# Graph attention in two layers: one multiplication of each step moved from VectorE to GpSimd

## The chip, the core and the metric

The kernel runs on one core of a Trainium2 chip. The core has five engines with queues of their own: TensorE (PE: matmuls; PEld: its weight loads), VectorE (DVE), ScalarE (ACT), GpSimd (POOL) and SyncE (SP, which only issues transfers). Each engine executes its instructions in the order of its own queue and waits at an instruction until the semaphores named there have been reached. The metric is the device time of one execution in microseconds (us); less is better.

## The reference

The input is a set of 2708 tokens of width 512 and a sparse, symmetric 0/1 matrix that says which tokens are neighbours. Two layers of the same form follow each other, each with weights of its own:

```python
q, k, v = h @ Wq.T + bq, h @ Wk.T + bk, h @ Wv.T + bv     # 8 heads of 64
scores  = einsum('nhd,mhd->hnm', q, k) / 8
scores  = where(adj + eye == 0, -1e9, scores)
ctx     = einsum('hnm,mhd->nhd', softmax(scores), v)
h1      = layer_norm(h + ctx @ Wo.T + bo)
h2      = layer_norm(h1 + relu(h1 @ W1.T + b1) @ W2.T + b2)   # 2048 inside
```

All values are float32. A token has few neighbours, at most some twenty, itself included, so almost all scores are masked.

## The kernel before

**Attention by lists.** The kernel does not form the matrix of scores. It first makes a list of neighbours for each token and sorts the tokens by the length of the list, so that the 22 tiles of 128 tokens have lists of bounded length (`CAPS`, from 22 slots in tile 0 to 3 in the last). A slot stands for one neighbour of each of the 128 tokens. The keys and values of all tokens of a layer lie in a table in HBM (`kv_d`), a row of 1024 numbers for each token, keys first.

**Steps.** A tile is worked off in steps of up to two slots. One step consists of these instructions:

- GpSimd issues one gather for each slot (`loads`, L1228; the instruction has the line L1099): 128 rows of the table come into a `kv` buffer.
- `weights` (L1134): VectorE multiplies the keys by the query (L1136, two slots in one instruction) and sums each head (L1142), which gives the scores `sc`.
- `weigh` (L1149): ScalarE takes the exponential of the scores (L1155, one instruction a slot), which gives the weights `p`. ScalarE multiplies the second slot's values with their weights, head by head, in eight instructions (L1162). VectorE multiplies the first slot's values with theirs in one instruction (L1168). In a tile's first step (`s0 == 0`) the products go to the sum `acc`; in every later step they stay in the `kv` buffer, and VectorE then adds them to `acc` (L1175).

When a tile is through, VectorE adds the two halves of the sum and reduces the weights (`sums`, L1179), and ScalarE divides (`divided`, L1206), which gives `cx`, the tile's context.

**Order of the work.** The order is written out by hand: each engine executes its instructions in the order in which the Python code emits them. `attend` (L1582) is a generator that emits a step at a time. In step k it first takes the next buffer, for which the gathers of step k+3 are emitted (`EARLY = 3`), then emits `weights` of step k and then `weigh` of step k-1, so that ScalarE has a step's time for the exponentials. In layer 1 a `kv` buffer is one of seven. `advance` (L1641) draws steps from this generator between the matmuls of another block, at a pace written in `PACE`, and `until` (L1653) draws what is still missing of a tile when its context is needed.

**Blocks.** Two tiles make a block; the feed-forward runs block by block (`feed_forward`, L1447), 16 stages `f` of four matmuls `pf` (L1494) and, three stages later, two matmuls `a` (L1467). During the feed-forward of one block the attention of later tiles is computed. At stage f = 10 TensorE transposes the context of the next block's first tile and at f = 11 that of its second (`flip`, `tp` L1273), projects both (`o`, L606), and VectorE adds the residual and normalises (`norm`, L1253; its reciprocal root `rd`, L1263, is on GpSimd). After the last stage VectorE adds the block's result `a` to the residual (L1532) and normalises again, and in layer 1 GpSimd scatters the rows to the output (`put`, L1062).

So GpSimd's queue holds gathers, the `rd` of every normalisation and the scatters, all in one order.

Of the kernel before, what the change touches and what calls it, by code (L numbers as in the profile page):

```python
# [480 lines left out]
def by_edges(ctx: ExitStack, tc: tile.TileContext, x, xT, adj, layers, out, redo):  # L481
# [9 lines left out]
    nc = tc.nc  # L491
# [142 lines left out]
    def size(g):  # L634
        return min(P, N - g * P)
# [472 lines left out]
    def asked(n, g):  # L1108

        r = size(g)  # L1110
        if g in own:
            return own.pop(g)
        if n == 0 and not all_made:
            return None
        q = at.tile([P, DM], F32, tag="q", name="q", bufs=QB)
        fetch(n, q, q_d[n], g)
        return q

    def chunks_of(g):
        S = CAPS[g]  # L1120
        k = (S + SLOTS - 1) // SLOTS
        cuts = [-(-S * i // k) for i in range(k + 1)]
        return [(g, a, b - a) for a, b in zip(cuts, cuts[1:])]

    class Tile:


        def __init__(self, g, q):
            self.g, self.r, self.q = g, size(g), q
            self.sc = at.tile([P, LIST, NH], F32, tag="sc", name="sc", bufs=2)  # L1130
            self.p = at.tile([P, LIST, NH], F32, tag="p", name="p", bufs=2)
            self.acc = None
# [16 lines left out]
        def weigh(self, kv, s0, c):  # L1149
            r, g, p = self.r, self.g, self.p  # L1150
            if s0 == 0:
                self.acc = at.tile([P, SLOTS, DM], F32, tag="acc", name="acc", bufs=2)
                self.wide = c
            for s in range(s0, s0 + c):
                nc.scalar.activation(  # L1155
                    p[:r, s, :], self.sc[:r, s, :], AF.Exp, bias=minus[:r, g, s : s + 1]
                )
            to = self.acc[:r] if s0 == 0 else kv[:r, :, DM:]
            for i in range(1, c):
                for h in range(NH):  # L1160
                    hd = slice(h * DK, (h + 1) * DK)
                    nc.scalar.activation(  # L1162
                        to[:, i, hd],
                        kv[:r, i, DM + h * DK : DM + (h + 1) * DK],
                        AF.Copy,
                        scale=p[:r, s0 + i, h : h + 1],
                    )
            nc.vector.tensor_tensor(  # L1168
                to[:, 0, :].rearrange("p (h d) -> p h d", d=DK),
                kv[:r, 0, DM:].rearrange("p (h d) -> p h d", d=DK),  # L1170
                p[:r, s0, :].unsqueeze(2).to_broadcast([r, NH, DK]),
                ALU.mult,
            )
            if s0:
                nc.vector.tensor_tensor(  # L1175
                    self.acc[:r, :c, :], self.acc[:r, :c, :], kv[:r, :c, DM:], ALU.add
                )
# [50 lines left out]
    def loads(n):  # L1228

        ready = []  # L1230
        for g, s0, c in (chunk for g in order for chunk in chunks_of(g)):
            r = size(g)
            kv = rows_of_keys(n)
            for s in range(s0, s0 + c):
                load = gather(kv[:r, s - s0, :], kv_d[n], idx[:r, g, s : s + 1])
                for move in written[n]:
                    tc.add_manual_dep(
                        load.ins,
                        move.ins.name,
                        mybir.DependencyInfo(  # L1240
                            mybir.DependencyClass.Sync, mybir.DependencyReason.DATA
                        ),
                        reason="every row of keys is in its place",
                    )
                written[n].clear()
            ready.append(kv)
            if len(ready) > EARLY:
                yield ready.pop(0)
        yield from ready
# [332 lines left out]
    def attend(n, got):  # L1582

        peak = small.tile([P, NT], F32, tag="peak", name="peak", bufs=1)
        nc.vector.memset(peak, 0.0)
        loaded = loads(n)
        steps = []
        for g in order:
            cuts = chunks_of(g)
            steps += [(g, s0, c, i, i + 1 == len(cuts)) for i, (_, s0, c) in enumerate(cuts)]  # L1590
            if g == order[1]:
                steps += [None] * 3
        steps += [None] * 3
        kv = next(loaded)
        yield 0.0
        q = asked(n, order[0])
        done = [None] * 3
        for k, step in enumerate(steps):
            if step:
                g, s0, c, i, last = step  # L1600
                if i == 0:
                    while q is None:
                        q = asked(n, g)
                        if q is None:
                            yield None
                    t, q = Tile(g, q), None
                if k > 0:
                    kv = next(loaded)
                t.weights(kv, s0, c)
                if q is None and g != order[-1]:  # L1610
                    q = asked(n, order[order.index(g) + 1])
                done.append((t, kv, s0, c, last))
            else:
                done.append(None)
            t3, t2, t1 = done[-4:-1]
            if t1:
                t1[0].weigh(*t1[1:4])
            if t2 and t2[-1]:
                t2[0].sums(peak)
            if t3 and t3[-1]:  # L1620
                got[t3[0].g] = t3[0].divided()
            yield c / SLOTS if step else 0.2
        nc.vector.tensor_reduce(flags[:, 4 + n : 5 + n], peak, AX.X, ALU.max)
        nc.vector.tensor_scalar(
            flags[:, 4 + n : 5 + n], flags[:, 4 + n : 5 + n], SAFE, None, ALU.is_le
        )
# [30 lines left out]

    got = {}
    ahead = attend(0, got)
    early = {}  # L1660

# [39 lines left out]
    for n in range(NL):  # L1701
        last = n == NL - 1
        nxt = None if last else Layer(n + 1, layers[n + 1])
        if n > 0:
            streamed = now.queries(order[10:16])
            got = {}
            ahead = attend(n, got)
            for _ in range(2):
                now.query(*pool.pop(0))
# [178 lines left out]
```

## Time and profile before

| what | value |
|---|---|
| time, median of 3 runs | 1846.8 us (1846.43 to 1847.19) |
| time of the profiled execution | 1846.72 us, of which the span from first to last instruction is 1844.6 us |
| granted TensorE clock, mean | 0.998 |
| layer 1 in the trace | from about 1085 us to the end |
| one block of feed-forward in layer 1 | 63.7 us |
| layer 1: gathers, mean | 210 of 1222 ns (1085 to 1780 us) |
| layer 1: L1168 on the first slot's values of a later step | 89 instructions, 689 ns |
| layer 1: L1168 of a tile's first step | 22 instructions, 697 ns |

The page of a profile has the engines' busy time first, then the costliest groups of instructions with mean duration and with what ended the idle time before them. Further views are asked of the trace: the waits of one engine in a stretch of time, the instructions of one engine in order of time (the timeline; its columns are start, duration, engine, line, operation, output<-inputs, shapes and, in brackets, idle time before and what ended it), and the busy time by stretches.

### The profile page before, as it was taken

The page shows a single profiled execution, that of the slowest core. Times are in us where ns is not written, and L with a number is a line of the kernel's source. Part 1 is how long each engine was busy: PE and PEld are TensorE (multiplying, and loading weights), DVE is VectorE, ACT ScalarE, POOL GpSimd, SP SyncE. Part 2 cuts the span into 40 slices and gives each one's busy share as a digit, 9 for nine tenths or more (in the row PEclk, how much of TensorE's full clock was granted, in tenths as well). Part 3 has the DMA queues.
Part 4 walks back from the last instruction along what each step waited for, and adds up shares of the span by engine and source line. Part 5 has one row for each costly group of instructions (what it writes and reads, how often), then busy time and mean ns, then how long its engine had stood idle before and what let it go on. Part 6 is the DMA issues. An engine that isn't in the chain of part 4 may idle for free.

```text
span 1844.6 us, 20998 instructions
## 1 busy us (share of the span) xinstructions
PE 1830.8 (99%) x6205; PEld 1095.4 (59%) x6205; DVE 1374.6 (75%) x2147; ACT 944.3 (51%) x3263; POOL 782.5 (42%) x745
## 2 busy tenths in 40 slices
PE   9999999999999999999999999999999999999997
PEld 4444456565666656566565544666666666666666
DVE  5886778787777777767774148877998988899842
ACT  5770445654446555555543113655665575566531
POOL 3234755544435434443431032444563545355302
PEclk9999999999999999999999999999999999999999
DMA  9997987654646455553631676845563755456300
GB/s 345 363 335 257 373 280 247 220 161 163 205 142 230 147 188 183 176 181 106 222 121 46 230 261 258 293 140 197 177 232 140 254 195 185 180 199 209 119 1 21
DMA packets 129829, 368.01 MB, mean 200 GB/s; under 512 B 14378, under 2 KB 32670, under 8 KB 129704
## 3 DMA queue, kind: packets, MB, share of 16 engines
q0 software_dynamic: 70608, 252.12, 39.6%
q1 hardware_dynamic: 50042, 93.64, 14.3%
q10 hardware_dynamic: 9054, 20.81, 2.9%
q8 instruction: 50, 0.82, 0.2%
q14 instruction: 75, 0.61, 0.1%
HBM read 315.84 MB, written 50.68 MB: 199 GB/s over the span
## 4 chain that ended last, share of the span: by engine, by line
PE 93%; DVE 3%; ACT 1%; issue 1%; DMA 1%; POOL 0%; SPq 0%; POOLq 0%; DVEq 0%
PE pf L1494 30%; PE a L1467 29%; PE o L606 8%; PE v L606 8%; PE k L606 8%; PE q L606 7%; PE tp L1273 3%; DVE sc L1142 1%; DVE kv L1136 1%; PE a L1482 1%; ACT kv L1162 1%; DVE acc L1175 0%; DVE kv L1168 0%; ACT cx L1206 0%; DMA kv<-kv_d,listed 0%
## 5 line engine op out<-in xcount | busy, mean ns | idle before, releaser
L1494 PE MATMUL pf<-hT,w 128*128 128x256 f32 (+1 forms) x2816 | 631.7, 372 | 0.1
L1494 PEld LDWEIGHTS pf<-hT,w 128*128 128x128 f32 x2816 | 518.3, 190 | 172.8 <-issue 107.5
L1099 POOL DMA_INDIRECT kv<-kv_d,listed x420 | 507.8, 1209 | 254.2 <-issue 108.7
L1467 PE MATMUL a<-w,ft 128*128 128x512 f32 x1312 | 611.2, 592 | 0.0
L1505 ACT ACTIVATE ft<-pf,b 128x256 f32<-128x256 f32 (+1 forms) x336 | 153.9, 461 | 412.0 <-PE pf L1494 411.9
L1467 PEld LDWEIGHTS a<-w,ft 128*128 128x128 f32 x1312 | 247.0, 190 | 187.2 <-issue 165.8
L1263 POOL TENSOR_TENSOR rd<-va,mhalf 128x1 f32<-128x1 f32 (+1 forms) x88 | 81.2, 922 | 565.4 <-DVE va L1261 565.4
L1162 ACT ACTIVATE kv<-kv,p 128x64 f32<-128x64 f32 x1232 | 311.0, 335 | 5.0
L1136 DVE TENSOR_TENSOR kv<-kv,q 128x1024 f32<-128x1024 f32 (+1 forms) x222 | 257.0, 1158 | 16.5 <-DMA q<-q_d,ident_i 13.0
L1142 DVE TENSOR_REDUCE sc<-kv 128x16 f32<-128x1024 f32 (+1 forms) x222 | 258.0, 1162 | 7.6
L1175 DVE TENSOR_TENSOR acc<-acc,kv 128x1024 f32<-128x1024 f32 (+2 forms) x178 | 205.3, 1153 | 76.5 <-ACT kv L1162 65.0
L1155 ACT ACTIVATE p<-sc,listed 128x8 f32<-128x8 f32 x420 | 104.3, 299 | 123.9 <-DVE sc L1142 112.9
L1168 DVE TENSOR_TENSOR kv<-kv,p 128x512 f32<-128x512 f32 (+1 forms) x178 | 123.1, 691 | 36.2 <-ACT p L1155 36.1
L606 PE MATMUL o<-wo,cT 128*128 128x512 f32 x336 | 148.4, 594 | 0.6 <-ACT cT L1278 0.6
L606 PEld LDWEIGHTS o<-wo,cT 128*128 128x128 f32 x336 | 62.2, 190 | 72.5 <-issue 60.9
L731 DVE MAX8 tops<-code 128x8 f32<-128x247 f32 (+2 forms) x242 | 78.6, 400 | 28.5 <-ACT code L726 28.2
L1267 DVE SCALAR_TENSOR_TENSOR h<-h,rd,ln_b 128x512 f32<-128x512 f32 (+1 forms) x88 | 66.1, 751 | 41.0 <-POOL rd L1263 41.0
L1206 ACT ACTIVATE cx<-acc,su 128x64 f32<-128x64 f32 (+1 forms) x352 | 88.2, 333 | 12.9 <-DVE su L1198 7.4
L1162 ACT ACTIVATE acc<-kv,p 128x64 f32<-128x64 f32 (+1 forms) x352 | 88.8, 334 | 1.4
L1560 ACT COPY kvs<-v 128x512 f32<-128x512 f32 (+1 forms) x22 | 12.9, 585 | 137.3 <-PE v L606 136.6
L726 ACT ACTIVATE code<-aj 128x1354 bf16<-128x1354 int32 (+1 forms) x44 | 72.9, 1719 | 16.0 <-POOL aj L720 11.3
L1429 DVE TENSOR_TENSOR h<-o,xb 128x512 f32<-128x512 f32 (+1 forms) x44 | 30.2, 687 | 63.6 <-PE o L606 46.5
(183 smaller groups left out, 1605.7 us busy)
## 6 DMA issues: line engine op xcount, KB each, us to landing
aj<-in_adj SPq DMA_DIRECT2D x42, 677.0 KB, 6.4
kv_d<-kvs ACTq DMA_DIRECT2D x21, 512.0 KB, 5.5
xg<-in_xT SPq DMA_DIRECT2D x19, 512.0 KB, 7.0
w<-in_W SPq DMA_DIRECT2D x16, 512.0 KB, 7.2
kv<-kv_d,listed POOLq DMA_INDIRECT x420, 6.0
zT_d<-zT SPq DMA_DIRECT2D x22, 256.0 KB, 4.1
xb_d<-h SPq DMA_DIRECT2D x21, 256.0 KB, 6.8
q<-q_d SPq DMA_DIRECT2D x21, 256.0 KB, 4.4
```

The lines of the kernel that those rows point to most:

```text
L606: nc.tensor.matmul(o[:r], xs(c), wm[:, c, :], start=(c == 0), stop=(c == NC - 1))
L1099: return nc.gpsimd.indirect_dma_start(out=to, out_offset=None, in_=table[:, :], in_offset=bass.IndirectOffsetOnAxis(ap=s, axis=0), bounds_ ...
L1136: nc.vector.tensor_tensor(kv[:r, :c, :DM], kv[:r, :c, :DM], self.q[:r].unsqueeze(1).to_broadcast([r, c, DM]), ALU.mult,)
L1142: nc.vector.tensor_reduce(self.sc[:r, s0 : s0 + c, :], kv[:r, :c, :DM].rearrange("p s (h d) -> p s h d", d=DK), AX.X, ALU.add,)
L1155: nc.scalar.activation(p[:r, s, :], self.sc[:r, s, :], AF.Exp, bias=minus[:r, g, s : s + 1])
L1162: nc.scalar.activation(to[:, i, hd], kv[:r, i, DM + h * DK : DM + (h + 1) * DK], AF.Copy, scale=p[:r, s0 + i, h : h + 1],)
L1168: nc.vector.tensor_tensor(to[:, 0, :].rearrange("p (h d) -> p h d", d=DK), kv[:r, 0, DM:].rearrange("p (h d) -> p h d", d=DK), p[:r, s0, : ...
L1175: nc.vector.tensor_tensor(self.acc[:r, :c, :], self.acc[:r, :c, :], kv[:r, :c, DM:], ALU.add)
L1206: nc.scalar.activation(cx[:r, hd], self.acc[:r, 0, hd], AF.Copy, scale=self.su[:r, h : h + 1])
L1467: nc.tensor.matmul(a[:r, cols], fts[f][:, c0 : c0 + r], self.w2[f // 2][:, f % 2, cols], start=(f == 0), stop=(f == NFC - 1),)
L1494: nc.tensor.matmul(pf[:, :w], self.w1[f // 2][:, c, f % 2 * P : f % 2 * P + P], hT[:, c, :w], start=(c == 0), stop=(c == NC - 1),)
L1505: nc.scalar.activation(ft[:, :w], pf[:, :w], AF.Relu, bias=self.b1[:, f : f + 1])
```

## The change

The multiplication of the first slot's values with their weights is given to GpSimd where the layer is the second one (`n` is 1) and the step is not the tile's first (`s0` is not 0). All else keeps its place in the code: the instruction is emitted at the same point of `weigh`, and the addition to `acc` on VectorE follows it. A tile now knows its layer.

```diff
-        def __init__(self, g, q):
-            self.g, self.r, self.q = g, size(g), q
+        def __init__(self, n, g, q):
+            self.n, self.g, self.r, self.q = n, g, size(g), q
...
-            nc.vector.tensor_tensor(
+            by = nc.gpsimd if self.n and s0 else nc.vector
+            by.tensor_tensor(
                 to[:, 0, :].rearrange("p (h d) -> p h d", d=DK),
                 kv[:r, 0, DM:].rearrange("p (h d) -> p h d", d=DK),
                 p[:r, s0, :].unsqueeze(2).to_broadcast([r, NH, DK]),
...
-                    t, q = Tile(g, q), None
+                    t, q = Tile(n, g, q), None
```

## Prediction

> **What bounds the kernel now.** I read the busy times first, then TensorE's waits in layer 1 (the only place that the edit touches), then the groups of the two engines that trade work.
>
> ```profile
> PE 1830.8 (99%) x6205; PEld 1095.4 (59%) x6205; DVE 1374.6 (75%) x2147; ACT 944.3 (51%) x3263; POOL 782.5 (42%) x745
> ```
> ```profile
> PE tp L1273 <- ACT cx L1206: 0.7, 1, 0.7
> PE o L606 <- ACT cT L1278: 0.6, 1, 0.6
> ```
>
> TensorE is busy for 99% of the span. The second fence is all that it waits for from 1085 to 1800 us: 1.3 us. So VectorE, though full, bounds nothing today except at two places, and relieving it can return about 1.3 us, under 0.1%. A measurement of this kernel can tell about 0.2% (3.7 us) from no change. The question is what the move does to the time at which contexts (cx) reach TensorE.
>
> ```profile
> L1099 POOL DMA_INDIRECT kv<-kv_d,listed x210 | 256.5, 1222 | 78.7 <-issue 44.3 <-DVE acc L1175 9.4 <-ACT p L1155 9.1
> L946 POOL TENSOR_TENSOR kvs<-kvs,bk 128x512 f32<-128x512 f32 x20 | 25.4, 1270 | 52.6 <-ACT kvs L942 47.4 <-issue 5.2
> L1168 DVE TENSOR_TENSOR kv<-kv,p 128x512 f32<-128x512 f32 x88 | 60.7, 689 | 3.9 <-ACT p L1155 3.8
> ```
>
> **Removed.** The third row (and one of 20 partitions): 89 multiplications on VectorE by 689 ns, 61 us. They lie under TensorE's work and are worth nothing by themselves, beyond the 1.3 us.
>
> **Added.** 89 multiplications on GpSimd. No row shows this one; the nearest is L946, GpSimd's float32 128x512 instruction with two inputs: 1270 ns, 1254 to 1297 in twenty. Bounds: 0.7 us if it ran as on VectorE; 2.5 us if on top of 1270 it also sat through a VectorE instruction of 1.2 us each time. I take 1.27, and expect an error upward rather than down, because VectorE was in one-input searches while L946 ran and is in two-input work here.
>
> **Where it lands in GpSimd's queue.** In step k the queue holds the gathers of step k+3, then the multiplication of step k-1, then the gathers of k+4, and so on. The multiplication waits for ScalarE's exponential, and the addition on VectorE (L1175) now waits for the multiplication. Until now GpSimd ran ahead of VectorE, held only by free buffers; now they are tied together step by step. Behind the multiplication stand gathers, the roots rd and the scatters. The gathers stay early enough: issued about three and a half steps (15 us) ahead, where a landing takes 6. The roots don't suffer: VectorE reaches a normalisation only after the addition that needed GpSimd's last multiplication. What counts is the length of a step, so I look at the densest stretch that ends at a waiting TensorE, tile 10 of the block (7, 10). GpSimd, then VectorE, from the timeline:
>
> ```profile
> 1299.35 1.53 POOL L1099 DMA_INDIRECT kv<-kv_d,listed  x1 [0.30 <-issue]
> 1303.45 0.99 POOL L1099 DMA_INDIRECT kv<-kv_d,listed  x1 [0.30 <-issue]
> 1304.74 1.62 POOL L1099 DMA_INDIRECT kv<-kv_d,listed  x1 [0.30 <-ACT p L1155]
> 1306.67 0.99 POOL L1099 DMA_INDIRECT kv<-kv_d,listed  x1 [0.30 <-issue]
> ```
> ```profile
> 1304.28 1.23 DVE L1175 TENSOR_TENSOR acc<-acc,kv 128x1024 f32<-128x1024 f32 x1
> 1305.42 1.22 DVE L1136 TENSOR_TENSOR kv<-kv,q 128x1024 f32<-128x1024 f32 x1
> 1306.67 1.22 DVE L1142 TENSOR_REDUCE sc<-kv 128x16 f32<-128x1024 f32 x1
> 1307.81 0.68 DVE L1168 TENSOR_TENSOR kv<-kv,p 128x512 f32<-128x512 f32 x1
> 1308.60 1.23 DVE L1175 TENSOR_TENSOR acc<-acc,kv 128x1024 f32<-128x1024 f32 x1
> ```
>
> VectorE's step is now 4.32 us (addition 1304.28 to addition 1308.60). A gather takes 0.99, but 1.62 at 1304.74, when VectorE is inside an addition until 1305.51; it ends 0.85 later. Over layer 1's timeline the 68 gathers that start beside no two-input VectorE instruction take 0.99; the other 142 average 1.33 and end 0.86 (median) after it. Gaps: 0.30 between gathers, 0.03 from gather to arithmetic, 0.18 from arithmetic to gather.
>
> [...] The trace shows one direction, GpSimd waiting. The other, VectorE held by a multiplication of 1.27, it shows nowhere. [...]
>
> **The step afterwards.** Cycle of GpSimd in a step: 0.18; a first gather that meets the addition just released, 1.95 (1.23 - 0.15 + 0.86); 0.30; a second, 0.99; 0.03; multiplication 1.27. That is 4.72 us. VectorE alone would need 4.32 - 0.68 = 3.6, so GpSimd now sets the step. Walked through tile 10 (additions of its four later steps; today at 1304.28, 1308.60, 1311.85, 1316.09): the scatter ends at 1299.04, three gathers run as now to 1304.44, multiplication to 1305.74, addition 1305.77; then every 4.72: 1310.49, 1315.21, 1319.93. The last is 3.8 us late: 1.5 from the start, 0.4 from each full step, 1.5 from the step of one slot, which today is short (3.25). The sum and the context follow it.
>
> ```profile
> 1321.66 2.01 ACT L1206 ACTIVATE cx<-acc,su 128x64 f32<-128x64 f32 x8
> 1325.91 0.60 PE L1273 MATMUL tp<-ident,cx 128*128 128x128 f32 x4
> 1327.12 2.41 PE L606 MATMUL o<-wo,cT 128*128 128x512 f32 x5 [0.60 <-ACT cT L1278]
> ```
>
> The context is done at 1323.67, and TensorE takes it at 1325.91: 2.24 us of room. 3.8 - 2.24 = 1.6 us of stall. The same gap for second tiles, read in the timeline: -1.4 and 2.25 in the blocks before, 5.9, 6.9, then 10.7 and more; first tiles have 12 and more. In the next block (6, 11) the room is 5.9 + 1.6; the lag carried in is about 3, tile 6 adds 2.7 (three full steps by 0.4 and one short one by 1.5), tile 11 adds 3.8 as tile 10 did, and VectorE's idle time, 64.0 - 57.8 = 6 us in a block, recovers some of it:
>
> ```profile
> 1290.00:1354.00 64.00, 63.40 (x223) 40.69 (x222) 57.84 (x78) 39.50 (x150) 33.17 (x27) 1.00 0.58 197
> ```
>
> I take half of it: 9.5 - 7.5 would be 2.0 with no recovery, none with all; 1.0. Blocks (8, 9), with 2.25 of room, and (18, 17), with none, have short tiles and many waits on TensorE or ScalarE in between; 1.5 together. Then 1 for VectorE held by the lock, 0.5 for a multiplication somewhat over 1.27 (four steps by 0.13), and -0.6 from the relief. Later blocks have room and cost nothing. Another deadline, the addition of a block's result to the residual (L1532), which must free TensorE's accumulators 7 us into the next block, has 1.7 to 3.9 us of room after three steps; three by 0.4 fits.
>
> Sum: 1.6 + 1.0 + 1.5 + 1 + 0.5 - 0.6 = 5.0 us. The profiled execution took 1846.72 us (span 1844.6 and 2.1 around it), as good as the median of 1846.8, so the time is **1852**, slower by 0.3%.
>
> **Rivals.** *Covered:* the multiplication costs about 1.1 or less, or finds GpSimd free earlier. The place is tile 10: its four cycles then sum to less than 2.24 us of lag plus today's time, which happens from a cycle of 4.72 - (1.6 / 4) = 4.3 down, a multiplication of 0.87, or from 1.1 with half of the starting delay of 1.5 absent. For it: GpSimd is busy only 33 us in that block of 64. Against: it is idle when VectorE is, too. Time 1847, not slower.
>
> [...]
>
> *Relief wins:* VectorE's additions start sooner, the 1.3 us of waits vanish and nothing else appears: 1845.5; over 0.2% isn't there to be had, since TensorE has no more idle time in layer 1.
>
> That the multiplications don't move is excluded: the condition holds for all 89.
>
> **How the numbers follow.** Stalls of a few us as worked out: 0.46 (its own range 1849 to 1860; about one in eight of it within 0.2%). Covered: 0.24. GpSimd the bound: 0.26. Relief: 0.04. The range must leave out 2 in 10: 1846 cuts off the relief and a little of the covered case, 1875 cuts off the upper half of the bound. Slower: 0.40 + 0.26 = 0.66; within 0.2%: 0.06 + 0.24 = 0.30; faster 0.04.
>
> **What would show it.** GpSimd's new row at 1.27 to 1.5 us a piece, 89 of them; a new wait of VectorE's addition on GpSimd, some tens of us in all; the gathers still short of delaying L1136; TensorE's waits at tp and o risen from 1.3 to about 6 us, at the contexts of tiles 10 and 11. Wrong would be: a row near 2 us, TensorE waiting in every block, or no wait at all.

## The result, and the profile after

The changed kernel takes 1862.93 us (median of 6 runs, 1860.9 to 1864.96) against 1846.78 us (6 runs beside it). The ratio is 1.0087, with a 95% interval of 1.0077 to 1.0097: 16.1 us slower, inside the predicted range and on the predicted side, but three times the 5.0 us of the sum. The profiled execution took 1860.9 us (span 1859.2), so its span has grown by 14.6 us, and these are what the readings below account for. From L1168 on, line numbers are one higher than before: the multiplication is L1169, the addition L1176, the transposition tp L1274, the eviction cT L1279, the relu ft L1506, the division cx L1207.

Busy times of the span, then TensorE's waits from 1085 to 1812 us (total, times, longest):

```profile
PE 1836.0 (99%) x6205; PEld 1095.7 (59%) x6205; DVE 1325.3 (71%) x2058; ACT 943.2 (51%) x3263; POOL 918.3 (49%) x834
```
```profile
PE o L606 <- ACT cT L1279: 6.1, 6, 3.3
PE pf L1495 <- ACT ft L1506: 2.8, 2, 1.5
PE q L606 <- DMA zT<-zT_d: 0.9, 1, 0.9
PE tp L1274 <- ACT cx L1207: 0.7, 1, 0.7
```

VectorE is busy for 49 us less and GpSimd for 136 more. TensorE's waits in layer 1 have gone from 1.3 to 10.5 us, and ScalarE ends nearly all of them: evictions (cT, which copy a transposed context out of TensorE's accumulator) and relus (ft), not contexts (cx). TensorE is also busy for 5 us longer with the same instructions; a part of that is a cost of its own, below.

GpSimd's groups from 1085 to 1800 us, and VectorE's longest wait in the same stretch:

```profile
L1099 POOL DMA_INDIRECT kv<-kv_d,listed x210 | 293.4, 1397 | 56.9 <-issue 45.7 <-POOL kv L1169 3.9 <-DMA kv_d<-kvs,ident_i 3.1
L1169 POOL TENSOR_TENSOR kv<-kv,p 128x512 f32<-128x512 f32 (+1 forms) x89 | 96.5, 1085 | 34.8 <-ACT p L1155 33.2
```
```profile
DVE acc L1176 <- POOL kv L1169: 75.0, 55, 3.4
```

The multiplication takes 1085 ns on GpSimd, not 1270 (L946, the row it was taken from, stays at 1268). VectorE's additions wait for it for 75 us, a wait that did not exist. The gathers have grown from 1222 to 1397 ns (210 of them: 37 us), because their timing has changed. In tile 10 this is seen instruction by instruction, GpSimd's timeline first, then VectorE's additions:

```profile
1307.12 1.06 POOL L1169 TENSOR_TENSOR kv<-kv,p 128x512 f32<-128x512 f32 x1
1308.34 1.99 POOL L1099 DMA_INDIRECT kv<-kv_d,listed  x1 [0.16 <-POOL kv L1169]
1310.64 1.00 POOL L1099 DMA_INDIRECT kv<-kv_d,listed  x1 [0.30 <-issue]
1311.67 1.05 POOL L1169 TENSOR_TENSOR kv<-kv,p 128x512 f32<-128x512 f32 x1
```
```profile
1308.22 1.23 DVE L1176 TENSOR_TENSOR acc<-acc,kv 128x1024 f32<-128x1024 f32 x1 [2.02 <-POOL kv L1169]
1312.75 1.22 DVE L1176 TENSOR_TENSOR acc<-acc,kv 128x1024 f32<-128x1024 f32 x1 [0.92 <-POOL kv L1169]
1317.29 1.23 DVE L1176 TENSOR_TENSOR acc<-acc,kv 128x1024 f32<-128x1024 f32 x1 [1.99 <-POOL kv L1169]
1321.82 0.69 DVE L1176 TENSOR_TENSOR acc<-acc,kv 128x512 f32<-128x512 f32 x1 [0.92 <-POOL kv L1169]
```

The multiplication ends, the addition that waited for it starts at once, and the gather that starts beside that addition takes 1.99 instead of 1.00 us. The cycle is 4.53 us, the same in all three steps. So the predicted mechanism is there. TensorE's waits lie elsewhere than predicted, though; ScalarE's and TensorE's timelines of the same place:

```profile
1327.38 2.00 ACT L1207 ACTIVATE cx<-acc,su 128x64 f32<-128x64 f32 x8
1329.29 0.45 ACT L1506 ACTIVATE ft<-pf,b 128x256 f32<-128x256 f32 x1
1329.82 0.49 ACT L1155 ACTIVATE p<-sc,listed 128x8 f32<-128x8 f32 x2
1330.34 2.02 ACT L1162 ACTIVATE kv<-kv,p 128x64 f32<-128x64 f32 x8
1332.27 0.46 ACT L1506 ACTIVATE ft<-pf,b 128x256 f32<-128x256 f32 x1
1332.62 1.11 ACT L1279 ACTIVATE cT<-tp,bv 128x128 f32<-128x128 f32 x4
```
```profile
1324.60 0.60 PE L1274 MATMUL tp<-ident,cx 128*128 128x128 f32 x4
1328.48 1.28 PE L1274 MATMUL tp<-ident,cx 128*128 128x128 f32 x4
1333.03 8.83 PE L606 MATMUL o<-wo,cT 128*128 128x512 f32 x16 [3.26 <-ACT cT L1279]
```

The eviction at 1332.62 is that of tile **7**, the block's first, whose context was transposed at 1324.60 and could have been evicted from 1325.2. It stands in ScalarE's queue behind tile 10's division and behind the exponentials and copies of one more step, and these came late because VectorE's scores did. TensorE needs tile 7's eviction first (o, 1333.03). What TensorE waits for is the queue. Tile 10's own context is late as well: it is done at 1329.38, 0.9 us after its transposition began, which therefore takes 1.28 us instead of 0.60. But that costs less than the eviction does.

The span's 14.6 us by place (the lag of each matmul behind the same one before): 0.4 ahead of layer 1; 0.9 at 1127 us (a wait at q for zT, the transposed tokens, which a transfer brings; in the kernels below with moved multiplications it is none in four and up to 3.3 us in one, and nothing ties it to the change); 1.25 at block (8, 9), half of it a transposition that does wait for its context (1.31 us instead of 0.60); 5.05 at block (7, 10); 2.55 at block (6, 11); 4.45 in the blocks after. Block (7, 10) holds more than its wait. Two windows of TensorE at that place (length, busy PE, PEld, DVE, ACT, POOL, granted clock, DMA share, GB/s):

```profile
1333.00:1338.00 5.00, 4.97 (x8) 2.19 (x9) 1.44 (x2) 2.13 (x8) 0.00 (x0) 0.66 0.26 93
1338.00:1343.00 5.00, 5.00 (x16) 2.69 (x16) 3.94 (x8) 0.00 (x0) 1.00 (x1) 1.00 0.00 0
```

After the wait the granted clock is at 0.5 from 1334.43 to 1337.84: 3.41 us, in which the matmuls o follow each other at 0.85 instead of 0.43 us. That adds 1.7 us to the 3.3 of the wait.

### The profile page after: what moved, and what is told of

Read it like the earlier page. It is cut to its first block, busy times and chain, and to the rows that moved or that the text cites. A ratio compares the mean times of both kernels' runs of the same rounds, so it can differ in the third digit from the quotient of the medians.

```text
span 1859.2 us, 20995 instructions
## 1 busy us (share of the span) xinstructions
PE 1836.0 (99%) x6205; PEld 1095.7 (59%) x6205; DVE 1325.3 (71%) x2058; ACT 943.2 (51%) x3263; POOL 918.3 (49%) x834
## 5 line engine op out<-in xcount | busy, mean ns | idle before, releaser
L1099 POOL DMA_INDIRECT kv<-kv_d,listed x420 | 543.9, 1295 | 233.0 <-issue 110.9
L1506 ACT ACTIVATE ft<-pf,b 128x256 f32<-128x256 f32 (+1 forms) x336 | 153.2, 460 | 391.1 <-PE pf L1495 377.7
L1176 DVE TENSOR_TENSOR acc<-acc,kv 128x1024 f32<-128x1024 f32 (+2 forms) x178 | 205.9, 1157 | 154.9 <-POOL kv L1169 75.0
L1136 DVE TENSOR_TENSOR kv<-kv,q 128x1024 f32<-128x1024 f32 (+1 forms) x222 | 262.4, 1182 | 16.6 <-DMA q<-q_d,ident_i 13.7
L1142 DVE TENSOR_REDUCE sc<-kv 128x16 f32<-128x1024 f32 (+1 forms) x222 | 257.9, 1162 | 7.6
L1169 POOL TENSOR_TENSOR kv<-kv,p 128x512 f32<-128x512 f32 (+1 forms) x89 | 96.5, 1085 | 34.8 <-ACT p L1155 33.2
L1207 ACT ACTIVATE cx<-acc,su 128x64 f32<-128x64 f32 (+1 forms) x352 | 88.2, 333 | 13.2 <-DVE su L1199 7.7
L1169 DVE TENSOR_TENSOR kv<-kv,p 128x512 f32<-128x512 f32 (+1 forms) x89 | 61.6, 692 | 32.3 <-ACT p L1155 32.3
```

The lines of the kernel that those rows point to most:

```text
L1099: return nc.gpsimd.indirect_dma_start(out=to, out_offset=None, in_=table[:, :], in_offset=bass.IndirectOffsetOnAxis(ap=s, axis=0), bounds_ ...
L1136: nc.vector.tensor_tensor(kv[:r, :c, :DM], kv[:r, :c, :DM], self.q[:r].unsqueeze(1).to_broadcast([r, c, DM]), ALU.mult,)
L1142: nc.vector.tensor_reduce(self.sc[:r, s0 : s0 + c, :], kv[:r, :c, :DM].rearrange("p s (h d) -> p s h d", d=DK), AX.X, ALU.add,)
L1169: by.tensor_tensor(to[:, 0, :].rearrange("p (h d) -> p h d", d=DK), kv[:r, 0, DM:].rearrange("p (h d) -> p h d", d=DK), p[:r, s0, :].unsqu ...
L1176: nc.vector.tensor_tensor(self.acc[:r, :c, :], self.acc[:r, :c, :], kv[:r, :c, DM:], ALU.add)
L1207: nc.scalar.activation(cx[:r, hd], self.acc[:r, 0, hd], AF.Copy, scale=self.su[:r, h : h + 1])
```

## The experiments

Unless said otherwise, each edit is to the changed kernel, and each ratio is to the kernel before on the same chip (1846.8 to 1847.4 us). `times(engine, a, b)` stands for the multiplication of heads a to b (b not included), with two more arguments for another place to write to and to read from. The excerpts of code leave out the lines around them.

### A tie without length, and length without a tie

GpSimd multiplies one head of eight; the addition still waits for it in every step.

```diff
-            by.tensor_tensor(... all heads ...)
+            if self.n and s0:
+                times(nc.gpsimd, 0, 1)
+                times(nc.vector, 1, NH)
+            else:
+                times(nc.vector, 0, NH)
```

> GpSimd multiplies one head of eight (64 columns, about 0.2 us), VectorE the other seven (about 0.62 us). The addition waits for GpSimd as in the changed kernel. A: GpSimd's step falls to 4.53 - 0.85 = 3.7 us, VectorE's own is 4.25: 1846 to 1849 us. If being tied step by step is what costs, whatever the duration: 1855 us or more.

1847.86 us, ratio 1.0004 (0.9995 to 1.0013). The addition waits 19.7 us for GpSimd, and TensorE 1.5 us at o. The tie between the engines alone costs nothing that can be measured; what GpSimd has to do between two ties does.

Then the opposite: VectorE keeps its multiplication, and GpSimd makes an additional one of the same size on keys that are no longer needed, which nothing waits for in its step.

```diff
+            if self.n and s0:
+                times(nc.gpsimd, 0, NH, keys, keys)   # keys: kv[:r, 0, :DM]
+            times(nc.vector, 0, NH)
```

> VectorE keeps the multiplication of the first slot in both layers. GpSimd does one of the same size at the same place of its queue, but on the dead keys' products in the same buffer, so that no addition waits for it. Theory A (the addition waits for GpSimd, whose step of 4.53 us is longer than VectorE's): VectorE runs in its own step of 4.32 us again, gathers have 15 us of lead, so 1847 to 1852 us; the additions' wait on GpSimd (75 us) is gone. Theory B (what costs is VectorE held by a GpSimd instruction that reads SBUF): VectorE's two-input rows grow at least as in the changed kernel (L1136 1260 ns for 1215) and it has the 61 us of multiplications on top: 1860 us or more.

1856.92 us, ratio 1.0048 (1.0031 to 1.0064), between what the two theories expected. VectorE's groups from 1085 to 1800 us, the addition, then its own multiplication:

```profile
L1182 DVE TENSOR_TENSOR acc<-acc,kv 128x1024 f32<-128x1024 f32 x77 | 107.4, 1395 | 17.0 <-ACT kv L1162 10.0
L1171 DVE TENSOR_TENSOR kv<-kv,p 128x512 f32<-128x512 f32 x88 | 78.0, 886 | 2.3 <-ACT p L1155 2.2
```

No addition waits for GpSimd, but additions take 1395 ns (1226 before) and multiplications 886 (689): 77 x 0.169 + 88 x 0.197 = 30 us more on VectorE. The reduction L1142, with one input, stays at 1220 ns. So the additions and multiplications became longer with GpSimd's arithmetic beside them, and without a tie that loses 9.6 us. (Late gathers are not the cause: L1136 waits 2.3 us for them, 3.5 before.)

### How much of the loss is that lengthening

The multiplication is left out for these steps; GpSimd fills the place of the product with zeros, twice, to take the same time without reading anything. (From a tile's second step on, the values of first slots are thus missing from the sums.)

```diff
+            if self.n and s0:
+                nc.gpsimd.memset(to[:, 0, :], 0.0)
+                nc.gpsimd.memset(to[:, 0, :], 0.0)
```

> In place of the multiplication GpSimd fills the first slot's values with zeros, twice (two times about 0.53 us), which reads nothing; the multiplication itself is left out in layer 1 from a tile's second step on, so the output is another one. Queue, duration and the addition's wait stay as in the changed kernel. A: 1858 to 1864 us, with a step of about 4.6 us in the dense stretch. B: VectorE isn't held any more (no L1136 above 1.25 us), so at least half of the 16 us goes: 1855 us or less.

1859.81 us, ratio 1.0067 (1.005 to 1.0084), inside what theory A expected. The two fills take 540 + 524 ns, as long as the multiplication. VectorE's key multiplication and addition:

```profile
L1136 DVE TENSOR_TENSOR kv<-kv,q 128x1024 f32<-128x1024 f32 x98 | 118.9, 1214 | 2.3 <-DMA kv<-kv_d,listed 2.3
L1184 DVE TENSOR_TENSOR acc<-acc,kv 128x1024 f32<-128x1024 f32 x77 | 94.3, 1225 | 101.9 <-POOL kv L1180 63.6 <-ACT kv L1162 33.9 <-issue 2.7
```

L1136 is back at the 1215 ns it had before (1260 in the changed kernel), so the fills do not lengthen it. Of the 16 us, 12.5 remain. The lengthening is thus worth 3 us here at most, and the two intervals overlap. By place, the profiled spans differ by 2.4 us, of which 0.7 arise ahead of layer 1, where the kernels are the same, and 0.8 at zT; 1.0 arises in the late blocks and none at the three blocks named above. The rest of the loss is there with fills in place of the multiplication.

### The length of GpSimd's step

Half of the heads on each engine, by the first edit with 4 in place of 1:

> GpSimd multiplies heads 0 to 3, VectorE heads 4 to 7, with an instruction each. Theory A (the length of GpSimd's step decides): GpSimd's multiplication takes about 0.55 us, its step 0.18 + 1.99 + 0.30 + 1.00 + 0.03 + 0.55 = 4.05 us, shorter than the 4.32 of before, so only the late start of a tile's first multiplication is left: 1848 to 1852. Theory B (VectorE held, in proportion to GpSimd's time in arithmetic): half of 16 us, 1855.

1850.78 us, ratio 1.0023 (1.0013 to 1.0032), inside what theory A expected. GpSimd's timeline in tile 10, from the multiplication of its third such step to that of the fourth:

```profile
1312.85 0.62 POOL L1171 TENSOR_TENSOR kv<-kv,p 128x256 f32<-128x256 f32 x1
1313.63 1.03 POOL L1099 DMA_INDIRECT kv<-kv_d,listed  x1 [0.16 <-issue]
1314.97 1.03 POOL L1099 DMA_INDIRECT kv<-kv_d,listed  x1 [0.30 <-issue]
1316.01 0.72 POOL L1171 TENSOR_TENSOR kv<-kv,p 128x256 f32<-128x256 f32 x1
```

The step is 3.16 us here; the 4.05 expected is met only by the tile's first (4.11), in which a gather of 2.00 us still meets the addition. Here the shorter multiplication is done before VectorE reaches the addition (1313.90), so the next gather is under way by then: 1.03 us. Half of the multiplication takes away three quarters of the loss. Tile 10 shows why: the step in which VectorE waits for GpSimd pays for the collision as well (4.11 us), and the one in which it doesn't pays nothing (3.16).

Twice the multiplication, the second on the product of the first, so that values are weighted twice:

```diff
+            if self.n and s0:
+                times(nc.gpsimd, 0, NH)
+                times(nc.gpsimd, 0, NH)
```

> GpSimd executes each moved multiplication twice, the second on the product of the first, so the values are weighted twice and the output differs. Theory A: GpSimd's step is 4.53 + 1.1 = 5.6 us, 1.3 above what the step was before, in some 4 steps of a tile and 8 of a block; that is 10 us a block against an idle time of VectorE of about 10 with the relief, so also the late blocks, which have room of 6 to 13 us, begin to stall: 1880 to 1920. Theory B (the tie alone costs, whatever GpSimd's time): 1863 to 1866.

1940.5 us, ratio 1.0511 (1.0494 to 1.0529): beyond the upper end of what was expected. The cycle is 5.66 us, as expected (additions of tile 10 at 1322.80, 1328.46, 1334.11, 1339.77), and VectorE's additions wait 181 us. TensorE's waits in layer 1, the four largest:

```profile
PE pf L1503 <- ACT ft L1514: 29.7, 16, 3.8
PE o L606 <- ACT cT L1287: 15.0, 7, 3.3
PE tp L1282 <- ACT cx L1215: 9.9, 4, 4.6
PE a L1476 <- DVE h L1541: 4.4, 4, 1.3
```

Half of these 59 us are at pf, at relus. The other 35 of the 94 us are in TensorE's busy time (1865.5 against 1830.8 us), with the granted clock down to 0.984 in the mean.

### When the multiplication starts

In layer 1 the exponentials, copies and GpSimd's multiplication of step k-1 are emitted at the top of step k, ahead of the gathers for step k+3. `weigh` is split for it: `spread` is that part, and the addition stays where it was.

```diff
+            if n and done[-1]:
+                done[-1][0].spread(*done[-1][1:4])   # L1155, L1162, L1169
...
                 if k > 0:
                     kv = next(loaded)                # gathers of step k+3
```

> In layer 1 the exponentials, ScalarE's copies and GpSimd's multiplication of step k-1 are emitted ahead of the gathers of step k+3 instead of behind them; VectorE's order is the same. GpSimd's step stays 4.53 us, but the multiplication no longer starts behind up to three gathers after a pause. A with a starting delay (1.6 of the 3.3 us by which tile 10 is late): the lag falls under the room of 2.24 us or little above it, 1848 to 1854 us. If the rate of GpSimd's queue alone decides: 1860 to 1864 us.

1852.33 us, ratio 1.0029 (1.0017 to 1.0042). The addition's wait for GpSimd falls from 75.0 to 42.1 us, and TensorE's at o from 6.1 to 2.2. At q it waits 3.3 us for zT, which is not explained; 3.7 of the 6.1 us by which this span is longer than that of before arise there, and only 0.1 at block (7, 10), where the changed kernel had 5.05. The step expected at 4.53 us became shorter too: in tile 10 the additions are 3.5, 3.8 and 4.5 us apart. At least two thirds of the loss depend on the multiplication standing behind gathers, which are not urgent (VectorE waits 3.5 us for them in all).

### Where it is lost

Moved only for the first ten tiles in order (blocks up to (6, 11), 35 multiplications), and only for the last twelve (54):

```diff
+            times(nc.gpsimd if self.n and s0 and order.index(g) < 10 else nc.vector, 0, NH)
...
+            times(nc.gpsimd if self.n and s0 and order.index(g) >= 10 else nc.vector, 0, NH)
```

> Moved only for the first ten tiles of the order (the blocks up to (6,11)): 35 of the 89 multiplications. Theory A (the loss is a stall where a context has little room; these ten tiles have rooms of -1.4, 2.2, 2.2 and 5.9 us): most of the loss stays, 1855 to 1859 (the lag built up to that point in the changed kernel is about 10 us), with TensorE's wait at o on cT of about 6 us. Theory B (the loss is spread over all multiplications, VectorE held or GpSimd full): 35/89 of 16 us, so 1853, with TensorE waiting in every block.

> Moved only for the last twelve tiles of the order, from block (5,12) on: the other 54 multiplications. Theory A: these contexts have 6.9 us of room and more, so the loss is small, 1847.5 to 1851, with TensorE waiting under 2 us at o on cT. Theory B (spread): 54/89 of 16 us, so 1857.

1856.17 us, ratio 1.0051 (1.0035 to 1.0068), and 1851.45 us, ratio 1.0027 (1.0017 to 1.0037). The first is in the middle of what theory A expected, with 5.2 us at o. The second is a miss at the edge: 4.65 us where 4.2 at most were expected. Together they make 14.0 of the 16.1 us. TensorE's waits in layer 1 with only the late tiles moved:

```profile
PE pf L1499 <- ACT ft L1510: 2.8, 2, 1.5
PE o L606 <- ACT cT L1283: 1.2, 3, 0.6
PE tp L1278 <- ACT cx L1211: 0.7, 1, 0.7
```

All late contexts arrive in time (tp waits as before), and yet TensorE loses 2.8 us at relus and 0.6 more at evictions. At the first of the relus, ScalarE's timeline, then TensorE's:

```profile
1447.21 0.49 ACT L1155 ACTIVATE p<-sc,listed 128x8 f32<-128x8 f32 x2 [1.04 <-DVE sc L1142]
1449.66 2.01 ACT L1211 ACTIVATE cx<-acc,su 128x64 f32<-128x64 f32 x8
1451.57 0.82 ACT L1510 ACTIVATE ft<-pf,b 128x256 f32<-128x256 f32 x2
```
```profile
1452.08 1.99 PE L1499 MATMUL pf<-hT,w 128*128 128x256 f32 x8 [1.25 <-ACT ft L1510]
```

The relu stands behind a division and behind exponentials that waited for VectorE's scores. In the kernel before, that division and the relus behind it come 4.4 us earlier (relus at 1447.18).

Then the four multiplications of tile 10 alone (`order.index(g) == 7`):

> Only the four multiplications of tile 10, the tile that the prediction walked through, are moved to GpSimd. Theory L (each late context loses by itself): the addition of the last step comes about 3 us late against a room of 2.25 and cT stands behind a step in ScalarE's queue, so TensorE waits 1 to 3 us at o: 1848 to 1851. Rival (the lateness is handed on from the tiles before, which are not moved here): 1846.5 to 1847.5.

1851.75 us, ratio 1.0026 (1.0016 to 1.0036): four instructions cost 4.8 us. That is theory L, but 0.75 us above its range: the wait of 3 us was expected at its upper end, and the slower clock behind it (0.61 in the mean from 1331.0 to 1335.4 us) was not. It is the cleanest look at the mechanism, since all else is as before. ScalarE's timeline, then TensorE's; and ScalarE's of the kernel before, for the same two instructions and the exponentials ahead of them:

```profile
1323.12 0.49 ACT L1155 ACTIVATE p<-sc,listed 128x8 f32<-128x8 f32 x2 [1.09 <-DVE sc L1142]
1325.58 2.02 ACT L1211 ACTIVATE cx<-acc,su 128x64 f32<-128x64 f32 x8
1327.85 0.48 ACT L1155 ACTIVATE p<-sc,listed 128x8 f32<-128x8 f32 x2
1328.37 2.03 ACT L1162 ACTIVATE kv<-kv,p 128x64 f32<-128x64 f32 x8
1330.66 1.11 ACT L1283 ACTIVATE cT<-tp,bv 128x128 f32<-128x128 f32 x4
```
```profile
1322.80 0.60 PE L1278 MATMUL tp<-ident,cx 128*128 128x128 f32 x4
1331.06 8.83 PE L606 MATMUL o<-wo,cT 128*128 128x512 f32 x16 [3.08 <-ACT cT L1283]
```
```profile
1319.21 0.49 ACT L1155 ACTIVATE p<-sc,listed 128x8 f32<-128x8 f32 x2 [0.81 <-DVE sc L1142]
1321.66 2.01 ACT L1206 ACTIVATE cx<-acc,su 128x64 f32<-128x64 f32 x8
1326.72 1.11 ACT L1278 ACTIVATE cT<-tp,bv 128x128 f32<-128x128 f32 x4
```

Tile 7's multiplications are not moved, its context is early as ever, and it is transposed at 1322.80. Its eviction comes 7.9 us later. From the exponential at 1323.12 on ScalarE is never idle, and the order and the distances are those of before (7.51 us from exponential to eviction before, 7.54 now); only the start is later, because it waited for VectorE's scores. So all of VectorE's lateness goes through to TensorE. Five kernels show how exactly: how much later tile 10's last addition starts, and how much later the first o, each minus the lag that TensorE already had at 1321 us:

| kernel | last addition, us late | first o, us late | after the matmuls o, us late |
|---|---|---|---|
| one head on GpSimd | 0.66 | 0.65 | 0.65 |
| half of the heads | 0.87 | 0.87 | 0.87 |
| tile 10 alone | 3.14 | 3.17 | 4.87 |
| two fills | 3.25 | 3.30 | 5.00 |
| the changed kernel | 3.16 | 3.34 | 5.04 |

No part of the lateness is absorbed. Where the wait was 3 us, 1.7 more are lost over the matmuls o: in the changed kernel at the halved clock (0.5 for 3.41 us), with tile 10 alone at the 0.61 named above. Three more kernels fit: 0.12 and 0.13 us with the early multiplication, 3.19 and 3.37 with ten tiles moved, 3.24 and 3.43 with the shifted step below.

### Two attempts on ScalarE's queue

The step of attention drawn at stage 10 of a block is drawn at stage 11, so that it is emitted behind both evictions; on the changed kernel, and on the kernel before as a control:

```diff
-    (0.0,) * 2 + (0.82,) * 9 + (0.0,) * 2 + (1.0,) * 3,
+    (0.0,) * 2 + (0.82,) * 8 + (0.0,) + (0.82,) + (0.0,) + (1.0,) * 3,
```

> The changed kernel with one number of PACE moved: in layer 1 the step of attention that was drawn at stage 10 of a block is drawn at stage 11, so that its exponentials and copies are emitted behind the evictions cT of both contexts and not ahead of them. Theory Q (TensorE waits at o because cT stands behind the exponentials and copies of a step in ScalarE's queue, and these wait for VectorE): TensorE's wait at o on cT falls from 6.1 to under 2 us, its clock stays at full speed in layer 1, and of the loss of 16 us about 6 go: 1855 to 1859. Theory C (it waits because the context itself is late): the wait moves to tp on cx and the time stays, 1861 to 1866.

> The kernel before with the same move of a step from stage 10 to stage 11, as a control. Both theories: 1846 to 1849, since TensorE waits for 1.3 us only in layer 1; over 1850 would mean that the move has a cost of its own, to be taken into account with the run above.

1874.72 us, ratio 1.0152 (1.0135 to 1.0169), and for the control 1847.07 us, ratio 1.0001 (0.9993 to 1.001). Neither theory had this. The wait at o in block (7, 10) is still 3.2 us, and the trace shows why the edit could not reach it: the order of ScalarE's work there is the same as in the changed kernel (division, exponentials, copies, then tile 7's eviction), because the step in front was drawn at a stage before 10. The edit puts a step behind the second eviction, and TensorE waits for the first. What it does is to start a step of every block one stage later: waits at pf rise to 7.7 us, at o to 9.5. The schedule before bears that at no cost, the changed one loses 12 us by it.

Two stages of the feed-forward share an accumulator in layer 1, each with half of its columns, so that three accumulators would have six places:

```diff
-                pf = ps_f.tile([P, DM], F32, tag="f", name="pf")
+                if f % 2 == 0 or self.n == 0:
+                    both = ps_f.tile([P, 2, DM // 2], F32, tag="f", name="pf")
+                pf = both[:, f % 2 if self.n else 0, :]
```

> The changed kernel, where in layer 1 two stages of the feed-forward share an accumulator pf (each writes half of its columns), so that TensorE may run further ahead of the relu ft on ScalarE. Theory Q (TensorE's waits at pf come from ft standing behind exponentials, copies and divisions in ScalarE's queue, with few accumulators to cover it): the waits at pf on ft, 3.0 us in the changed kernel, vanish, 1859 to 1861. Rival (the accumulators are not the limit): 1862.5 to 1864, or more if a shared accumulator makes TensorE wait for the other half.

1916.49 us, ratio 1.0375 (1.0358 to 1.0392). TensorE now waits for relus 40 times, 46.7 us (2 times, 2.8 us in the changed kernel), at 1159.07 us, for one, 0.56 us. The edit put in a wait of its own, in the author's reading for the relu of the other half, and says nothing on whether more accumulators would cover relus that come late.

Emitting the first tile's transposition and eviction a stage earlier, which its early context would allow and which goes at the cause, was not tried.

## Why the prediction was right in kind and a third in size

The side was foreseen by its mechanism: GpSimd's step becomes longer than VectorE's, and tile 10 comes late by about as much as worked out. The size was not. 1863 lies above the 1849 to 1860 that the prediction gave to stalls "as worked out"; the whole range holds it only because it reached up to 1875 for GpSimd as the bound, which did not happen. Its sign, that waits at tp and o rise from 1.3 to about 6 us at tiles 10 and 11, came true (6.8 us, most of it in those two blocks), but in part by luck: TensorE waits there for the first tile's eviction, and not for the contexts of tiles 10 and 11.

**What bounds, and what is removed: right.** The relief of VectorE (61 us of multiplications, 49 us net) bought nothing, and the 0.7 us at tp stayed. The -0.6 of the sum was not there.

**The multiplication: 1.27 predicted, 1.085 measured**, with a median of 1.055. The error was expected upward and was downward. The *Covered* rival had its threshold near it (1.1, with half of the starting delay absent). At 1.085 nearly all of the starting delay was there (1.37 of 1.5 us), and nothing was covered. At 0.73 (half of the heads), below that rival's 0.87, 4 us were still lost, and at 0.52 (one head) none that can be measured: with no room, the threshold lies lower than was worked out.

**The cycle: 4.72 predicted, 4.53 measured**, term by term: 0.16 and 0.30 as read, 1.99 for the gather beside the addition (1.95), 1.00, 0.03, and 1.055 for 1.27. **The last addition: 3.8 late predicted, 3.2 measured.** Up to here the sum was good, and a little too dear.

**The room: the step that failed.** "The context is done at 1323.67, and TensorE takes it at 1325.91: 2.24 us of room. 3.8 - 2.24 = 1.6 us of stall." The room was measured from tile 10's context to its transposition. The deadline that binds is the eviction of tile 7, in ScalarE's queue behind tile 10's work and one step more, and there the room was nil: TensorE was already waiting 0.60 us for it, in the last line of the fence that the prediction itself showed. The stall is then all of 3.2 and not 1.6; the table above shows it one for one. Counted from the context, only 3.2 - 2.25 = 0.9 us would have been due.

**Missing: the clock.** In the changed kernel the stall of 3.3 us is followed by 3.41 us at a granted clock of 0.5, 1.7 us more. Block (7, 10) cost 5.05 instead of 1.6 us; with tile 10 alone, 4.8.

**Block (6, 11): 1.0 predicted, 2.55 measured**, with the same error of room: 5.9 us from context to tp, but 2.8 at the eviction of tile 6. In the kernel before this starts at 1387.69, an o can follow 0.4 us later, and the first o runs at 1390.94. In the changed kernel the eviction comes 4.9 us later, TensorE's lag of 7.6 us taken off, and 4.9 - 2.8 = 2.1 us are lost at that o. **Blocks (8, 9) and (18, 17): 1.5 predicted, 1.25 measured**, all in the first.

**"Later blocks have room and cost nothing": wrong.** They cost 4.5 us in the changed kernel, and 4.65 when they alone are moved, with contexts 4 us early and more. The relus and evictions of those blocks stand in the same queue. The rooms were misread at the end, too: the last block's second tile, 0, has 6.2 us and not 10.7 or more, and the wait of 1.5 us at a relu is for one that stands behind its division.

**VectorE held: 1 us predicted; at most 3 measured, 1.0 by place** (the run with two fills against the changed kernel). No run shows the lock that the sum's 1 us is put down to; what the runs show is longer instructions. With the multiplication L1136 takes 1260 ns, with fills, which write only, 1214 (1215 before). In the changed kernel L1136 and L1176 together grew by 6 us only (134.0 + 103.3 against 128.5 + 102.7), as VectorE often stands waiting while GpSimd multiplies (75 us). Untied, these rows and VectorE's own multiplications grew by 36 us. In the other direction, a gather's instruction took 1.99 us beside an addition and 1.00 alone.

**The deadline at L1532 and the gathers: right.** TensorE doesn't wait there in the changed kernel, and L1136 waits 2.8 us for gathers (3.5 before).

**GpSimd as the bound** did not happen, at 1.085 us. Had it, the range's upper end of 1875 was probably too low: for a multiplication of 1.8 us, which no run has, a straight line between 1.085 (16 us) and the doubled multiplication (94 us) gives an estimate of 67 us.

Sum by place: 5.05 + 2.55 + 1.25 + 4.45, and 1.3 ahead of these blocks (0.4 before layer 1 and 0.9 at q, which nothing here ties to the change), is 14.6 us of span.

## What to carry to other kernels

A room is not the distance from a result to its consumer; it is read at every instruction queued behind the late one, on each engine that it passes through. Look first at the waits that the bounding engine already has: where it waits 0.6 us today, there is no room, whatever the gap at another instruction says. And before work goes to an engine that is "half idle", lay out its step with the wait that starts it: here two gathers stood in front, and the moment at which it released its partner made the next gather twice as long (1.99 us instead of 1.00).

## What the runs showed of the hardware

- **A stall of TensorE of about 3 us can cost half as much again.** In the changed kernel the wait of 3.26 us at o is followed by a granted clock of 0.5 for 3.41 us, in which the matmuls o are 0.85 us apart instead of 0.43: 1.7 us more. With tile 10 alone the wait is 3.08 us, the granted clock is 0.61 in the mean from 1331.0 to 1335.4 us, and the 16 matmuls o take 8.83 us as in the changed kernel. With the early multiplication the waits at q are 3.3 us, 2.9 the longest, and no more than 3.7 us are lost there; the granted clock of that execution is 0.999 in the mean (0.998 before). What makes the difference was not shown.
- **GpSimd's multiplication and VectorE's multiplication of the keys took longer beside each other.** In the last tile, where no gathers are left, this is seen alone; VectorE's timeline and GpSimd's, of the kernel with late tiles moved:

```profile
1761.28 1.22 DVE L1180 TENSOR_TENSOR acc<-acc,kv 128x1024 f32<-128x1024 f32 x1
1762.41 2.06 DVE L1136 TENSOR_TENSOR kv<-kv,q 128x1024 f32<-128x1024 f32 x1
```
```profile
1761.77 1.62 POOL L1171 TENSOR_TENSOR kv<-kv,p 128x512 f32<-128x512 f32 x1 [2.75 <-ACT p L1155]
```

  The multiplication starts inside the addition and takes 1.62 us, 0.57 more than its 1.05; L1136, which comes next, takes 2.06 and not 1.22 (its length in the same tile before). So VectorE loses 0.84 us to the instruction that was to save it 0.69.
- **GpSimd's times for 128x512 float32.** A multiplication with eight weights a token spread over 512 values takes 1.055 us in the median, an addition of two full operands 1.27 (L946); whether the operation or the operands make the difference was not tested. A half and an eighth of the multiplication take 0.62 and 0.30 in most steps of tile 10 (0.73 and 0.52 in the mean of layer 1). A fill takes 0.53.
